# Relative scores of both halves ahead of the attention, norms and slot weights in another order: one change to a twelve-layer decoder kernel

## The chip, the core and the metric

The kernel runs on one core of one Trainium2 chip. The core has a matrix engine (PE, TensorE, with PEld for its weight loads), three engines for elementwise work (DVE or VectorE, ACT or ScalarE, POOL or GpSimd), and SP, which here only issues transfers. Each engine works through its own instructions in a fixed order and waits, where it must, for another engine or for a transfer. PE, DVE, ACT and POOL compute on SBUF; PE writes its products to PSUM[...]. The metric is the device time of one execution in microseconds, lower is better; a kernel is compared by the median of its runs.

## The reference

The input `x` is 16 sequences of 64 tokens of 128 features, 1024 rows. Twelve sublayers follow one another, each added to its input and normalized over the features:

```python
x = _layernorm(x + _L2_ffn_ref(x, ...), axis=-1)    # sw: best of 16 experts, and a shared one
x = _layernorm(x + _L3_attn_ref(x, ...), axis=-1)   # at3: relative positions, causal
x = _layernorm(x + _L3_xattn_ref(x, ctx_1024, ...), axis=-1)  # xa3: attention to ctx
x = _layernorm(x + _L3_ffn_ref(x, ...), axis=-1)    # tt: best two of 8 experts
```

These four are the last ones, and the change lies among them. The attention with relative positions has 16 heads of 8 features. To the product of queries and keys it adds the product of the queries with a table of relative positions, read at a skew: row `q`, column `k` takes entry `k - q + n - 1`.

```python
scores = jnp.einsum('bhqd,bhkd->bhqk', q, k)
scores = scores + jnp.einsum('bhld,lrd->bhlr', q, rel_emb[rel_idx])
scores = jnp.where(causal[None, None], -jnp.inf, scores)
attn = jax.nn.softmax(scores / np.sqrt(HD), axis=-1)
```

The last layer routes each token to its two best experts and weights the two outputs with a softmax of the two logits:

```python
topk_logits, topk_idx = jax.lax.top_k(logits, TOP_K)
w = jax.nn.softmax(topk_logits, axis=-1)
h = gelu(jnp.einsum('th,ehi->tei', xt, W1) + b1)
y = jnp.einsum('te,teh->th', gates, jnp.einsum('tei,eih->teh', h, W2) + b2)
```

## The kernel before

**Halves.** The 1024 rows are two halves `h` of 512, each as four tiles of 128 rows. `self.xt[h]` holds the rows with tokens on the partitions, `self.x[h]` the transpose. Each sublayer ends in `close`: statistics on DVE (L195, L197), the inverse deviation, and a normalization (L206) into a new `xt`. For most layers POOL computes the inverse deviation (L201, L204). For `sw` it is `inverse_deviation`, eleven small DVE steps (L176 to L183) with a scratch tile `pd_sw` in PSUM. `close` returns `flip`: it fills PE with some `keep_busy` matmuls, transposes `xt` on PE (L224) and copies the result to `x[h]` on ACT (L226).

**Order.** A planner places the instructions. For each engine it takes the earliest instruction in program order that its own model of time finds ready; so program order is a priority, and the order on the chip is fixed when the kernel is built. A tile is a named buffer of a pool; a tag with `bufs=n` has n places, and the (n+1)th tile of the tag waits until a place is free. Pools are opened and closed by stage.

**Two streams.** A stage of attention layers is written as two generators, one for each half. `side_by_side` runs the first `lead` steps of half 0 and then steps of both in turn. A step ends at a `yield`. In `attention` the first step of `at3` computes the queries and keys (`at_pq`, `at_pk`, copied by ACT at L429, keys spread over masks by POOL at L441), calls `relative`, computes the values, and does `weights` of the first of four units. A unit is a quarter of the half's scores, 128 by 1024. `weights` computes the scores on PE (L480, with the mask added at L491), adds the relative scores (L533), takes the maximum (L536), subtracts it (L537) and exponentiates on ACT (L540). The following steps take the next units; `turn` transposes a unit (L551), `weigh` multiplies it with the values (L572).

**Relative scores.** For each of the four units `relative` computes the product with the table (`at_rs`), copies it from PSUM (ACT, L659), writes it to memory in two transfers (L663), and reads it back at a skew in four (L673), all through SP's queue. What comes back is a tile of tag `got` with `bufs=4`, which `weights` then uses as its scores and `turn` frees.

**The routed layers.** In `switch_ffn` (`sw`) and `top2_ffn` (`tt`) `place` computes a slot for each token and choice. `tiles_in_step` then works through tiles of 128 slots: POOL gathers the rows of a tile (`fetch`, L1336), PE transposes them (`turn`), `first`, `flip` and `second` are the two products of the tile's expert and what lies between. `between(k)` is called at the head of step k, from k = -1 on. In `tt` it is `weigh`: at k = 0 it computes each slot's weight `ws` and target row `outs` with ten DVE steps, one of ACT (L1572), 16 matmuls (`tt_pw`, L1582) and seven DVE sums; `second(0)`, which is called at k = 2, is the first to use them. After the tiles of `sw`, POOL gathers the tokens' rows (`sw_back`, eight transfers), and for each half DVE adds them to `base` (L1473), and `close(...)()` normalizes and transposes at once. After those of `tt` two reads for each half (`tt_back`, L1640), two additions (L1644) and `close` follow, and the four tiles of each half are stored by SP (L211).

**Where the stages meet.** `run` opens the attention stage's pools after `switch_ffn` has closed its own:

```python
        self.switch_ffn()
        with self.work_pools("a3", {8: 3, 4: 8, 2: 8}):
            self.side_by_side(self.second_stream, 2)
        self.top2_ffn()
```

Of the kernel before, what the change touches and what calls it, by code (L numbers as in the profile page):

```python
# [11 lines left out]
F32 = mybir.dt.float32  # L12
# [9 lines left out]
P = 128  # L22
B, S, D = 16, 64, 128
# [14 lines left out]
class Kernel:  # L38
# [146 lines left out]
    def close(self, pool, h, y, tag, shift=False, ones=0):  # L185

        nc = self.nc
        stats = self.lnp.tile([P, 4, 6], F32, tag=f"stats{h}", name=f"stats_{tag}{h}")  # L190
        mv = self.lnp.tile([P, 4, 2], F32, tag=f"mv{h}", name=f"mv_{tag}{h}")
        rstd = self.lnp.tile([P, 4], F32, tag=f"rstd{h}", name=f"rstd_{tag}{h}")
        xt = self.xp.tile([P, 4, D], F32, tag=f"xt{h}", name=f"xt_{tag}{h}", bufs=1 + h)
        for i in range(4):
            nc.vector.bn_stats(stats[:, i, :], y[:, i, :])  # L195
        for i in range(4):
            nc.vector.bn_aggr(mv[:, i, :], stats[:, i, :])  # L197
        if tag == "sw":
            self.inverse_deviation(rstd, mv, self.psum(pool, f"pd_{tag}{h}"))
        else:  # L200
            nc.gpsimd.tensor_tensor(  # L201
                rstd, mv[:, :, 1], self.eps.to_broadcast([P, 4]), ALU.add
            )
            nc.gpsimd.tensor_tensor(rstd, rstd, self.minus.to_broadcast([P, 4]), ALU.pow)  # L204
        for i in range(4):
            nc.vector.tensor_scalar(  # L206
                xt[:, i, :], y[:, i, :], mv[:, i, 0:1], rstd[:, i : i + 1], ALU.subtract, ALU.mult
            )
            if tag == "tt":
                at = h * HALF + i * P  # L210
                nc.sync.dma_start(  # L211
                    out=self.out.rearrange("b s d -> (b s) d")[at : at + P, :], in_=xt[:, i, :]
                )
        self.xt[h] = xt

        def flip():
            ps = self.psum(pool, f"px_{tag}{h}")
# [190 lines left out]
    def attention(  # L408
# [4 lines left out]
        nc = self.nc  # L413
        work, psc, pt = self.aw, self.psc, self.pt
# [101 lines left out]
        km = km or keys(x)  # L516
        rels = self.relative(tag, rel, q, h, scores) if rel else None
        v = values()
        y = self.new_y(tag, h) if wo is None else None
# [122 lines left out]
    def relative(self, tag, rel, q, h, scores):  # L642
# [12 lines left out]
        for u in range(2):  # L655
            for gp in range(2):
# [3 lines left out]
                mem = self.scratch.tile([2, P, row], F32, tag=f"rel{h}{u}{gp}", name=f"{tag}_mem{h}{u}{gp}")  # L660
                got = work.tile([P, 2, 2, 4, S], F32, tag="got", name=f"{tag}_rel{h}{u}{gp}", bufs=4)
                for pr in range(2):
# [720 lines left out]
    def switch_ffn(self):  # L1383
        nc, tc, x = self.nc, self.tc, list(self.x)
        E = 16
        with (
# [81 lines left out]
            for i in range(8):  # L1468
                self.gather(back[i // 4][:, i % 4, :], self.sw_out, slot[:, i : i + 1])
            for h in range(2):  # L1470
                y = self.new_y("sw", h)
                for i in range(4):
                    nc.vector.tensor_tensor(y[:, i, :], base[h][:, i, :], back[h][:, i, :], ALU.add)  # L1473

                    if h == 0:
                        for n in range(4):
# [3 lines left out]
                            )  # L1480
                self.close(pt, h, y, "sw", ones=4 - 2 * h)()

# [17 lines left out]
    def top2_ffn(self):  # L1500
        nc, tc = self.nc, self.tc
        E = 8
        with (
# [49 lines left out]
            def weigh(k):  # L1553
                if k != 0:
                    return
# [57 lines left out]
            def second(k, e, hid):  # L1613
# [18 lines left out]
                "tt", work, pt, self.tt_in, ids, first, flip, second, weigh, 20  # L1632
            )
            for h in range(2):
                y = self.new_y("tt", h)
                last = self.xt[h]
                for c in range(2):
# [7 lines left out]
                    last = y  # L1645
                self.close(pt, h, y, "tt")

# [119 lines left out]
    def second_stream(self, h):  # L1767
# [3 lines left out]
        def third():  # L1771
# [11 lines left out]
            ),  # L1783
            third,
        )
        self.score(h, "tt", "tt_wg", 8)

    def side_by_side(self, stream, lead):

        ahead, behind = stream(0), stream(1)  # L1790
        for _ in range(lead):
            next(ahead)
        running = [ahead, behind]
        while running:
            running = [half for half in running if next(half, self) is not self]

    def run(self, out):
# [20 lines left out]
        with self.work_pools("a3", {8: 3, 4: 8, 2: 8}):  # L1818
            self.side_by_side(self.second_stream, 2)
        self.top2_ffn()  # L1820
# [191 lines left out]
```

## Time and profile before

| | us |
|---|---|
| median of 3 runs | 896.4 (886.66 to 896.52) |
| profiled execution | 871.75 |
| its span, first to last instruction | 869.8 |
| from the last tile of `sw` to the first product of `at3` (633 to 652.3) | 19.3 |
| `at3` until PE is full (652.3 to 692) | 39.7 |
| from the last product of `xa3` to the first of `tt` (770 to 795.2) | 25 |
| from the last product of `tt` to the end (849 to 869.8) | 21 |

The durations that follow come from the profiled execution, so a sum is set against 871.75 and its span of 869.8. The three runs are longer than it by 1.7 to 2.8%.

How a line of the timeline is read: start, duration, engine, line, operation, output `<-` inputs, shapes of the output and of the first input, and how many instructions were merged (`x4`); in brackets the idle time of that engine before it, and what ended it. `PE` times are those of pipelined matmuls and overlap. A transfer on `SPq` is listed with the time in which SP issued it, not with its landing. Clock is the TensorE clock that was granted, as a share of full speed.

### The profile page before, as it was taken

How to read it: one execution, taken by the hardware profiler on the slowest of the kernel's cores; microseconds unless marked ns; L12 is line 12 of the kernel's file. 1: busy time of each engine (PE TensorE's matmuls, PEld its weight loads, DVE VectorE, ACT ScalarE, POOL GpSimd, SP SyncE). 2: the span in 40 equal slices, each digit the busy share in tenths (PEclk: the TensorE clock that was granted, in tenths of full speed). 3: DMA queues.
4: the chain of work that ended last, by engine and by line, in shares of the span. 5: the costliest groups of instructions: out<-in, count | busy, mean ns of one | idle time of the engine just before them, and what ended most of it. 6: DMA issues, size and time to landing. Idle time of an engine off the chain costs nothing.

```text
span 869.8 us, 17379 instructions
## 1 busy us (share of the span) xinstructions
PE 717.0 (82%) x7045; PEld 455.8 (52%) x7045; DVE 481.7 (55%) x1103; ACT 354.9 (41%) x584; POOL 254.0 (29%) x289
## 2 busy tenths in 40 slices
PE   6777979878888699789996999977947999967990
PEld 2333646555545466546573557644633565744770
DVE  4556466574665745447525766544542565656563
ACT  2223547445454444445551445522304554522330
POOL 2314135070432703130305220016151111025732
PEclk7878989889999998989996989988977799978995
DMA  7900000000000000140000000051115625031102
GB/s 277 273 1 25 2 1 2 14 1 2 1 2 1 1 2 2 40 155 2 2 2 0 1 2 2 2 151 48 50 41 148 198 54 184 2 122 37 53 25 83
DMA packets 34504, 43.65 MB, mean 50 GB/s; under 512 B 7524, under 2 KB 26469, under 8 KB 33784
## 3 DMA queue, kind: packets, MB, share of 16 engines
q1 hardware_dynamic: 32344, 38.26, 14.1%
q0 software_dynamic: 2080, 4.26, 1.7%
q8 instruction: 58, 0.95, 0.5%
q14 instruction: 22, 0.18, 0.1%
HBM read 34.31 MB, written 11.61 MB: 53 GB/s over the span
## 4 chain that ended last, share of the span: by engine, by line
PE 51%; DVE 18%; POOL 9%; issue 6%; ACT 4%; DMA 4%; SPq 1%; DVEq 0%; POOLq 0%; ACTq 0%
PE xa_sc L480 5%; PE xa_av L572 4%; PE xa_pt L551 3%; PE sw_pe L151 2%; PE at_sc L480 2%; PE lb_qk L151 2%; DVE lb_t L818 2%; PE at_av L572 2%; PE xa_sc L491 2%; DMA at_mem<-at_rsb 2%; DVE lb_t L832 2%; PE xa_pt L156 2%; PE at_pt L551 1%; PE lb_pf L868 1%; PE lb_pw L151 1%
## 5 line engine op out<-in xcount | busy, mean ns | idle before, releaser
L536 DVE TENSOR_REDUCE xa_mx<-xa_sc 128x16 f32<-128x1024 f32 x40 | 48.7, 1218 | 63.8 <-PE xa_sc L491 41.4
L838 POOL TENSOR_TENSOR lb_t<-lb_t,lb_t 128x1024 f32<-128x1024 f32 x16 | 37.7, 2357 | 99.4 <-DVE lb_t L832 95.2
L554 ACT COPY xa_eT<-xa_pt 128x512 f32<-128x512 f32 x80 | 45.5, 587 | 40.8 <-PE xa_pt L551 40.0
L540 ACT ACTIVATE xa_e<-xa_e 128x1024 f32<-128x1024 f32 x40 | 42.3, 1058 | 37.2 <-DVE xa_e L537 37.1
L480 PE MATMUL xa_sc<-xa_km,xa_q 32*64 32x256 f32 x640 | 55.2, 404 | 0.7 <-ACT xa_q L431 0.5
L551 PE MATMUL xa_pt<-const,xa_e 128*128 128x128 f32 x320 | 48.8, 280 | 1.8 <-ACT xa_e L540 1.8
L441 POOL TENSOR_SCALAR xa_km<-xa_k,const 128x512 f32<-128x512 f32 x40 | 27.1, 695 | 79.3 <-ACT xa_k L429 46.0
L537 DVE TENSOR_TENSOR xa_e<-xa_sc,xa_mx 128x1024 f32<-128x1024 f32 x40 | 48.7, 1217 | 2.1
L551 PEld LDWEIGHTS xa_pt<-const,xa_e 128*128 128x128 f32 x320 | 40.3, 145 | 13.1 <-ACT xa_e L540 3.7
L572 PEld LDWEIGHTS xa_av<-v,xa_eT 128*64 128x64 f32 x1280 | 40.5, 138 | 8.2 <-issue 6.1
L572 PE MATMUL xa_av<-v,xa_eT 128*64 128x18 f32 (+1 forms) x1280 | 44.2, 209 | 0.0
L156 PEld LDWEIGHTS <-ones_b 128*128 128x128 bf16 x255 | 24.8, 104 | 36.4 <-issue 19.9
L151 PE MATMUL lb_qk<-w,lb_hs 128*128 128x512 f32 x64 | 35.8, 686 | 8.5 <-DVE lb_t L832 4.8
L480 PEld LDWEIGHTS xa_sc<-xa_km,xa_q 32*64 32x64 f32 x640 | 24.7, 136 | 19.9 <-issue 12.8
L814 DVE TENSOR_REDUCE lb_ss<-lb_t 128x16 f32<-128x1024 f32 x16 | 19.5, 1217 | 27.9 <-ACT lb_t L811 27.9
L201 POOL TENSOR_TENSOR rstd_xa<-mv_xa,eps 128x4 f32<-128x4 f32 x8 | 1.6, 201 | 112.2 <-DVE mv_xa L197 112.2
L156 PE MATMUL xa_pt<-ones_b 128*128 128x512 bf16 x80 | 30.2, 390 | 0.0
L862 POOL TENSOR_TENSOR lb_t<-lb_t,lb_rs 128x1024 f32<-128x1024 f32 x16 | 30.1, 1904 | 0.0
L868 PE MATMUL lb_pf<-const,lb_t 128*128 128x128 f32 x128 | 20.1, 312 | 9.4 <-POOL lb_t L862 9.3
L480 PE MATMUL at_sc<-at_km,at_q 32*64 32x256 f32 x256 | 22.5, 452 | 5.2 <-DVE at_rel L533 3.7
L533 DVE TENSOR_TENSOR at_rel<-at_rel,at_sc 128x1024 f32<-128x1024 f32 x8 | 9.7, 1212 | 29.2 <-DMA at_mem<-at_rsb 16.4
L554 ACT COPY at_eT<-at_pt 128x512 f32<-128x512 f32 x32 | 17.6, 586 | 19.3 <-PE at_pt L551 13.4
(474 smaller groups left out, 1715.0 us busy)
## 6 DMA issues: line engine op xcount, KB each, us to landing
sw_gu<-in_sw_gu SPq DMA_DIRECT2D x4, 1024.0 KB, 8.3
at_mem<-at_rsb SPq DMA_DIRECT2D x16, 256.0 KB, 2.9
at_rel<-at_mem SPq DMA_DIRECT2D x32, 128.0 KB, 3.0
w<-in_w SPq DMA_DIRECT2D x1, 3114.0 KB, 12.2
sw_dn<-in_sw_dn SPq DMA_DIRECT2D x4, 512.0 KB, 7.0
tt_w<-in_tt_w SPq DMA_DIRECT2D x2, 1024.0 KB, 8.6
tt_b<-in_tt_b SPq DMA_DIRECT2D x1, 2048.0 KB, 7.1
sw_in<-in_zeros SPq DMA_DIRECT2D x1, 1472.0 KB, 11.6
```

The source lines that it names most:

```text
L151: self.nc.tensor.matmul(out, lhsT, rhs, start=n == 0, stop=n == len(pairs) - 1)
L156: self.nc.tensor.matmul(out, self.ones_b, self.ones_b.unsqueeze(1).to_broadcast([P, 4, P]), start=True, stop=True)
L480: nc.tensor.matmul(sc[64 * j : 64 * j + 64, gg, at : at + 256], q[r, t], part[r, :, t] if local else part[r, :, :], start=not masked or (p ...
L536: nc.vector.tensor_reduce(mx, scored, AX.X, ALU.max)
L537: nc.vector.tensor_tensor(e3, scored, mx.unsqueeze(2).to_broadcast([P, 16, S]), ALU.subtract)
L540: nc.scalar.activation(e3, e3, AF.Exp, scale=scale)
L551: nc.tensor.transpose(ps[:, bass.ts(n, P)], blocks[:, bass.ts(n, P)], self.g("ident"))
L554: nc.scalar.copy(eT[:, gg, :], ps)
L572: nc.tensor.matmul(av[64 * j : 64 * j + 64, pr, hp, :, :], eT[:, gg, at : at + 64], v[:, b, hp, :, :], start=True, stop=True,)
L838: nc.gpsimd.tensor_tensor(t1, t1, t2.rearrange("p t n d -> p t (n d)"), ALU.add)
L862: nc.gpsimd.tensor_tensor(t3, t3, rs[:, bass.ts(r, 16)].unsqueeze(2).to_broadcast([P, 16, 64]), ALU.mult)
L868: nc.tensor.transpose(ps[:, c, :], t1[:, t, bass.ts(c, P)], ident)
```

## The change

Five edits, as one change.

1. `close` is split into `moments` (statistics and inverse deviation) and `normalize` (the normalization and `flip`). Both keep their last instruction, `self.measured` and `self.normed`. `flip` takes the pool of its PSUM tile as an argument.
2. After `sw` half 1 is ended inside `tc.issue_after(self.normed.ins)`: every DVE instruction of half 1 that is traced there comes after half 0's last normalization on DVE. Half 1's `flip` is no longer run there. It is handed to the second stream, which runs it at the start of half 1's first layer, with the new stage's PSUM pool.
3. In `attention` a step ends after `relative`, and `side_by_side` takes a number `both` of steps that both halves do first. With `both=1` in the second stream, queries, keys and relative scores of half 1 come ahead of values and `weights` of half 0. The tag `got` has five places.
4. In `tt` `weigh` does its work at k = 2, right ahead of `second(0)`.
5. At the end of `tt` the moments of both halves come first, then, on DVE behind the last `bn_aggr` of half 1, both normalizations with their stores.

```diff
+        mv, rstd = self.moments(pool, h, y, tag)
+        return self.normalize(pool, h, y, tag, mv, rstd, shift, ones)
+
+    def moments(self, pool, h, y, tag):
...
         for i in range(4):
-            nc.vector.bn_aggr(mv[:, i, :], stats[:, i, :])
+            self.measured = nc.vector.bn_aggr(mv[:, i, :], stats[:, i, :])
...
+        return mv, rstd
+
+    def normalize(self, pool, h, y, tag, mv, rstd, shift=False, ones=0):
+        nc = self.nc
+        xt = self.xp.tile([P, 4, D], F32, tag=f"xt{h}", name=f"xt_{tag}{h}", bufs=1 + h)
         for i in range(4):
-            nc.vector.tensor_scalar(
+            self.normed = nc.vector.tensor_scalar(
...
-        def flip():
+        def flip(pool=pool):
...
         rels = self.relative(tag, rel, q, h, scores) if rel else None
+        if rel:
+            yield
         v = values()
...
-                got = work.tile([P, 2, 2, 4, S], F32, tag="got", name=f"{tag}_rel{h}{u}{gp}", bufs=4)
+                got = work.tile([P, 2, 2, 4, S], F32, tag="got", name=f"{tag}_rel{h}{u}{gp}", bufs=5)
...
-            for h in range(2):
+            def end(h):
                 y = self.new_y("sw", h)
...
-                self.close(pt, h, y, "sw", ones=4 - 2 * h)()
+                return self.close(pt, h, y, "sw", ones=4 - 2 * h)
+
+            end(0)()
+
+            with tc.issue_after(self.normed.ins):
+                flip = end(1)
+
+            self.flips = [None, lambda: flip(self.pt)]
...
             def weigh(k):
-                if k != 0:
+                if k != 2:
                     return
...
+            made = []
             for h in range(2):
                 y = self.new_y("tt", h)
...
-                self.close(pt, h, y, "tt")
+                made.append((h, y, "tt", *self.moments(pt, h, y, "tt")))
+            with tc.issue_after(self.measured.ins):
+                for half in made:
+                    self.normalize(pt, *half)
...
             third,
+            flip=self.flips[h],
         )
...
-    def side_by_side(self, stream, lead):
+    def side_by_side(self, stream, lead, both=0):
...
         ahead, behind = stream(0), stream(1)
+        for _ in range(both):
+            next(ahead)
+            next(behind)
...
-            self.side_by_side(self.second_stream, 2)
+            self.side_by_side(self.second_stream, 2, 1)
```

## The prediction

> **What bounds the kernel now.** I read the page first: the busy times and the chain that ended last.
>
> ```profile
> PE 717.0 (82%) x7045; PEld 455.8 (52%) x7045; DVE 481.7 (55%) x1103; ACT 354.9 (41%) x584; POOL 254.0 (29%) x289
> PE 51%; DVE 18%; POOL 9%; issue 6%; ACT 4%; DMA 4%; SPq 1%; DVEq 0%; POOLq 0%; ACTq 0%
> ```
>
> TensorE is the bound on the whole, but the change touches only stages around the two routed layers, so the share over the span says little. The second view is busy time by stage (us; then PE, PEld, DVE, ACT, POOL; clock, DMA share, GB/s).
>
> ```profile
> 633.00:652.00 19.00, 10.32 (x46) 8.24 (x46) 9.64 (x54) 0.91 (x2) 11.50 (x15) 0.68 0.11 29
> 652.00:668.00 16.00, 11.69 (x138) 5.35 (x138) 0.46 (x1) 7.21 (x10) 3.14 (x5) 0.82 0.36 106
> 668.00:692.00 24.00, 21.30 (x210) 11.66 (x211) 13.02 (x12) 12.11 (x16) 2.98 (x4) 0.71 0.70 204
> 692.00:712.00 20.00, 19.37 (x271) 13.80 (x271) 16.45 (x19) 10.17 (x16) 0.00 (x0) 0.95 0.33 95
> 849.00:870.00 21.00, 0.00 (x0) 0.00 (x0) 7.36 (x29) 0.00 (x0) 4.03 (x6) 0.55 0.26 82
> ```
>
> From 692 on PE is full at clock 0.95; from 633 to 692 it is not, and its clock is 0.68 to 0.82. Those 59 us, and the tail after 849, are where order can be worth something. The third view, the timeline, says who waits there.
>
> ```profile
> 650.00 1.11 DVE L206 TENSOR_SCALAR xt_sw<-y_sw,mv_sw,rstd_sw 128x128 f32<-128x128 f32 x4
> 652.31 2.08 PE L151 MATMUL at_pq<-x_sw,w 128*128 128x512 f32 x2 [0.68 <-ACT x_sw L226]
> 667.54 1.22 DVE L533 TENSOR_TENSOR at_rel<-at_rel,at_sc 128x1024 f32<-128x1024 f32 x1 [16.43 <-DMA at_mem<-at_rsb]
> 671.52 1.22 DVE L533 TENSOR_TENSOR at_rel<-at_rel,at_sc 128x1024 f32<-128x1024 f32 x1 [0.24 <-DMA at_rel<-at_mem]
> 675.74 1.22 DVE L533 TENSOR_TENSOR at_rel<-at_rel,at_sc 128x1024 f32<-128x1024 f32 x1 [0.50 <-DMA at_rel<-at_mem]
> 688.98 1.22 DVE L533 TENSOR_TENSOR at_rel<-at_rel,at_sc 128x1024 f32<-128x1024 f32 x1 [9.49 <-DMA at_rel<-at_mem]
> ```
>
> VectorE waits 16.4 us for the first relative scores, and 9.5 us again at 688.98. That fourth addition belongs to half 1: it stands in DVE's order ahead of half 0's last one (690.74), and its scores were still in memory. The queue that carries them is SP's:
>
> ```profile
> 674.23 3.43 SPq L673 DMA_DIRECT2D at_rel<-at_mem  x4
> 681.50 2.56 SPq L663 DMA_DIRECT2D at_mem<-at_rsb  x4
> 684.16 5.21 SPq L673 DMA_DIRECT2D at_rel<-at_mem  x8
> ```
>
> Half 0 is read back by 677.66. Then SP is empty for 3.8 us, since half 1's product (L480, 678.27) and its copy (L659, 680.48) come only then. From half 1's first write to its addition: 688.98 - 681.50 = 7.5 us.
>
> **The change part by part.** Sums are against the profiled run, 871.75 us (span 869.8 and 1.95 around it). The median of the three runs shown is 896.4, 2.8% longer; I carry the saving over as a share.
>
> *Norms behind the first routed layer.* Now DVE mixes half 1's additions, which wait 0.39, 0.46 and 0.99 us for gathers, into half 0's chain. Afterwards half 0 goes first. Its last addition is at 641.05, its statistics end at 641.95. Eleven steps of inverse_deviation at a pitch of 0.20 (648.19 to 649.80 in eight pitches) reach 644.2, four normalizations (1.11) 645.3, where they now end at 648.08. Half 1 then pays four additions and four statistics (0.27 each, 2.2), aggregates 0.45, eleven steps 2.2: 650.15, and its normalization ends at 651.3 (now 651.11). So half 1 loses 0.2 and half 0 wins 2.8. What is it worth? at_pq of half 0 starts now at 652.31, held by the copy of x_sw of half 1, which it does not read: half 0's copy ended at 649.10. PE's order alone would have released it at 651.64, when half 1's transposes end. So the first tile of the new PSUM pools waits for the last use of the closed ones. Afterwards the transposes and copy of half 1 belong to the new pool, but the scratch of its inverse_deviation still belongs to the old: at_pq can start at about 650.3. Value 2.0; bounds 5.9 (646.4, if only half 0's copy counts) and 0. I take the row's behaviour, a wait for the whole pool.
>
> The moved flip issues two keep_busy, four transposes (1.24) and one copy (0.59); they go behind half 0's product, on PE and ACT. SP and POOL get nothing of it. Here a rule speaks against the change: the Trainium skill, "TensorE: Matmul & The Clock Gate", section "HAM oscillation — how this bites in real kernels", warns of PE gaps above about 3.4 us, after which the array runs at half rate. The deferral leaves PE idle from about 645.9 to 650.3, 4.4 us, where now keep_busy and transposes fall. The row: at_pq takes 2.08 now, xa_pq of the same form 1.12 at 720.64, so it is already at half rate; a gap costs nothing more. By the rule taken alone the pair pq, pk would lose 1.9 us; by the row 0. I take 0.
>
> *Relative scores of both halves first.* For half 1 these move ahead of half 0's values and scores: on PE pq and pk (1.0 to 2.0 each) and four products (0.65 warm, 1.0 cold each); on ACT the copies of q and k (0.59 each) and four of 0.97; on POOL base (1.26) and four km (2.98); on SP 8 writes and 16 reads at 0.61, 14.6 us of queue. Nothing else stands in SP until 714.89 (tt_w) or in POOL until 713.92, so those two delay nobody. ACT does: from 655.4, eight copies of 0.97 and three of 0.59 last until 665.0, the PSUM slots go to half 0's scores then, 1.7 us later they are ready: 666.7. Its first scores come back from memory 2.0 us earlier than now, 665.5. So the first addition is at 666.8, now 667.54. The following two at the larger of DVE's 3.75 per unit (three passes of 1.22 and gaps) and SP's cadence (671.52 to 675.74, 4.2): 670.6 and 674.4, all hidden under transfers.
>
> Then half 1: half 0's reads end on SP at 675.7 (677.66 less 2.0). Half 1's data have been waiting since 665, so its write follows at once; with the same 7.5 us the addition is at 683.2 instead of 688.98. That is 5.8 earlier, the 2.0 included, so 3.8 of its own. What is late next is the same addition's transfer (DVE would be free at 678.2). The remaining reads of half 1 need a buffer freed by half 0's transposes (five buffers instead of four: only the first is free at once); those transposes are at about 672 to 685, and SP has only half 1's own reads behind the wait. From there on the stage is full of PE work (row 692:712) and keeps what it has won.
>
> Second rule, same place: "DMA: Bandwidth & Descriptors", section "Issuing engines are not separate DMA queues", calls a sequencer's time to initiate a DMA "usually small relative to the DMA itself". Were that so here, half 1's unit would go out beside half 0's, land near 675, and DVE would go on at 678.2: 10.8 instead of 5.8. The rows say 0.61 of issue against a median of 3.0 to landing, and 48 of them in one ordered queue: 29 us. I take the row, and keep 10.8 as an end. The other end is a loss of 3: if PE does half 1's products strictly ahead, half 0's scores end near 670.7 and the first addition is 3.3 later.
>
> *Slot weights behind the first tiles.* The 16 matmuls of tt_pw (2.02 us) stand before the first tile's product.
>
> ```profile
> 793.17 2.02 PE L1582 MATMUL tt_pw<-tt_wof,tt_at_row 128*128 128x138 bf16 x16 [1.74 <-issue]
> 795.20 1.65 PE L151 MATMUL tt_ph<-tt_w,tt_xs 128*128 x2
> ```
>
> The first product can start at 793.2 instead (tile 1's gather, issued at 789.66, lands by 792.5 at the 2.85 of tile 0; PE's own issue of 1.74 stays). PE pays the matmuls later, at up to 2.02 cold, half of it warm, partly in the 0.79 us in which PE waits for the first Gelu at 798.61. Ends: 0, if the same gaps are filled as now, and 2.0; value 1.0. The DVE steps of weigh (3 copies, 2 subtractions, 5 products of 0.53, 7 sums) move with it, beside tiles that leave DVE 40% free (33.2 of 54 us busy in 795:849).
>
> *Norms at the end.*
>
> ```profile
> 859.25 1.11 DVE L206 TENSOR_SCALAR xt_tt<-y_tt,mv_tt,rstd_tt 128x128 f32<-128x128 f32 x4 [1.22 <-POOL rstd_tt L204]
> 859.63 6.05 SPq L211 DMA_DIRECT2D out<-xt_tt  x8
> 863.55 1.11 DVE L206 TENSOR_SCALAR xt_tt<-y_tt,mv_tt,rstd_tt 128x128 f32<-128x128 f32 x4 [1.40 <-POOL rstd_tt L204]
> ```
>
> DVE idles 1.22 for POOL's power and normalizes half 0 before half 1's second addition. Afterwards half 1's statistics end at 859.85, POOL's 1.3 us end at 861.2, its normalization starts at 861.25: 2.3 earlier. Half 0's starts at 859.9, so the first of eight stores leaves at 860.25; at SP's pitch of 0.46 the last leaves at 863.5, now 865.3. So SP's queue limits it: 1.8 (between 0.5 and 2.3).
>
> Sum: 2.0 + 3.8 + 1.0 + 1.8 = 8.6 us. 871.75 - 8.6 = 863.2, a ratio of 0.990; 896.4 x 0.990 = 887.5.
>
> **The rivals.** *The queue keeps it (20%).* SP's issue, not the late product, sets half 1's landing: reads that wait for a buffer stretch it, and the 3.8 is nothing. For: only one spare buffer. Against: 3.8 us of empty SP. 4.8 us remain: 866.9, or 891.5.
>
> *PE fills up (20%).* Half 1's scores land early, the 9.5 us stall goes almost wholly and PE comes warm into the stage: 10.8, with 2.0 and 2.3 of the last two parts, and some 2 us of matmuls at full clock (at_sc of 1.98 at 668 to 690 against 1.09 at 694.61, four of them): 17. 854.7, or 879.
>
> *A read that waits stands before others (13%, slower).* If SP's order puts a read of half 1, which needs half 0's first buffer, ahead of half 0's own last reads, SP stops until half 0's first transposes (about 676) and every later unit costs a full 7.5 instead of 4.2: three units, 10 us, against 5.8 + 2.8 of gain. Net 1.4 to 4 slower: about 873 to 876, 898 to 900. It decides from a wait of some 3 us per unit. Against it: program order has all of half 0's reads first.
>
> That the change does not do what it says is likely only for the slot weights: an idle PE may take the same matmuls first. It is in their lower end.
>
> **How the numbers follow.** The forecast has 47%, the rivals 20, 20 and 13. Runs of the same kernel lie between 886.66 and 896.52, so 2% (about what a measurement can tell from no change) is 18 us: the forecast is within it. Faster by over 2%, under 878.5: half of "PE fills up" and a little of the forecast through spread, 0.2. Slower by over 2%, over 914: only if the last rival is worse than worked out, 0.06. The range takes in all four cases with the spread on either side: 869 to 902.
>
> **What would show it.** Right: at_pq near 650; at_rs of half 1 before the first at_sc; SP without a hole between half 0's last read and half 1's first write; the DVE wait of 9.5 down to about 5; tt_ph ahead of tt_pw; stores of the output in one row of eight. Wrong: at_pq still at 652 or already at 646; the first L533 later than 668; SP waiting for transposes amid half 0's reads; the stage from 692 on longer than now.

## The result and the profile after

The changed kernel takes 878.98 us (median of 4 runs, 875.16 to 884.41) against 894.02 (886.66 to 896.52) for the kernel before. The ratio on record is 0.9882, 95% interval 0.9833 to 0.9930; the quotient of the two medians, 0.983, lies at its lower end. Measured again with more runs (experiment 5) the ratio is 0.9909 (0.9886 to 0.9933), about 8 us of 889. The changed kernel is faster by about 1%, no more than single runs of one kernel differ by. Ratios leave out executions that took over 1.5% longer than the fastest of their kernel; the profiled executions of experiments 3 and 10 are of that kind.

The two profiled executions say the opposite at first sight: the span is 882.4 us, and it was 869.8. The busy times of the changed kernel:

```profile
PE 722.0 (82%) x7043; PEld 455.5 (52%) x7045; DVE 483.1 (55%) x1103; ACT 354.3 (40%) x584; POOL 254.9 (29%) x289
```

The work is the same (for the kernel before see the prediction), so the 12.6 us lie in waits and in the clock. A good part of them lies in layers that the change doesn't touch. Busy time from 50 to 100 us, of the kernel before and then of the changed one (us; PE, PEld, DVE, ACT, POOL; clock, DMA share, GB/s):

```profile
50.00:100.00 50.00, 41.90 (x401) 23.41 (x398) 26.52 (x56) 17.86 (x35) 12.78 (x16) 0.84 0.04 12
```

```profile
50.00:100.00 50.00, 42.10 (x320) 22.32 (x317) 25.77 (x54) 15.62 (x31) 12.67 (x15) 0.70 0.04 11
```

In the same 50 us PE got through 320 matmuls instead of 401, at a granted clock of 0.70 instead of 0.84. When the first gather of `sw_back` starts, the changed kernel is already 9.3 us behind (643.14 against 633.86), before anything of the change has run. So two profiled executions can't be set against each other by their spans. From here on every time is counted from an event close by: G is the start of the first gather of `sw_back`, T that of the first gather of `tt_got`.

| us | before | after | exp. 5: after again |
|---|---|---|---|
| G to `at_pq` | 18.5 | 15.6 | 15.8 |
| G to the first addition of relative scores | 33.7 | 37.6 | 34.4 |
| G to the fourth | 55.1 | 49.2 | 48.8 |
| G to the fifth | 56.9 | 53.9 | 53.5 |
| G to the eighth | 73.9 | 70.3 | 70.5 |
| G to half 1's `y_at` | 96.3 | 94.2 | 92.9 |
| T to the first `tt_ph` | 6.9 | 4.1 | 4.2 |
| T to the first scatter | 16.4 | 19.5 | 19.3 |
| T to the last scatter | 61.3 | 69.2 | 69.0 |
| last scatter to the end of the span | 20.2 | 17.9 | 18.3 |

The 8 us in the row "T to the last scatter" don't come from the change: with the slot weights in the old place it was 68.3 to 70.1 in experiments 1, 2, 4 and 6, and 61.3 to 61.4 only in this profile of before and in that of experiment 11 (last section).

Busy time by stage in the changed kernel, the stretches that answer to those shown of before:

```profile
642.28:661.28 19.00, 10.11 (x43) 7.51 (x44) 10.41 (x54) 0.98 (x2) 12.38 (x15) 0.70 0.11 29
661.28:677.28 16.00, 13.10 (x134) 5.72 (x135) 0.00 (x0) 8.64 (x12) 5.38 (x8) 0.71 0.51 153
677.28:701.28 24.00, 20.97 (x279) 12.28 (x272) 17.96 (x17) 13.20 (x18) 0.00 (x0) 0.93 0.77 228
```

The second stretch holds more transfers (153 GB/s, it was 106) and no VectorE at all; in the third VectorE is busy 18.0 of 24 us, where it was 13.0. That is the change at work: relative scores go out early, and the additions then follow closely. Who waits, from the timeline of the changed kernel (first, fourth and fifth addition only):

```profile
658.50 0.16 DVE L183 SCALAR_TENSOR_TENSOR rstd_sw<-pd_sw,rstd_sw 128x4 f32<-128x4 f32 x1
658.76 2.04 PE L151 MATMUL at_pq<-x_sw,w 128*128 128x512 f32 x2 [3.78 <-issue]
680.72 1.22 DVE L544 TENSOR_TENSOR at_rel<-at_rel,at_sc 128x1024 f32<-128x1024 f32 x1 [20.91 <-DMA at_mem<-at_rsb]
692.34 1.22 DVE L544 TENSOR_TENSOR at_rel<-at_rel,at_sc 128x1024 f32<-128x1024 f32 x1 [2.37 <-DMA at_rel<-at_mem]
697.00 1.22 DVE L544 TENSOR_TENSOR at_rel<-at_rel,at_sc 128x1024 f32<-128x1024 f32 x1
```

`at_pq` starts 0.10 us after the last step of half 1's inverse deviation has ended (658.66), as was worked out. The first addition is late: half 1's product and its copies stand ahead of half 0's first scores. The wait of 9.5 us before the fourth is down to 2.4 here, and to 5.0 in experiment 5, where the first addition came earlier.

The slot weights stand behind the first products of two tiles now, and most of the gain is gone a few microseconds later:

```profile
799.49 1.44 PE L151 MATMUL tt_ph<-tt_w,tt_xs 128*128 x2
803.49 1.21 PE L1600 MATMUL tt_pw<-tt_wof,tt_at_row 128*128 128x138 bf16 x16
811.65 2.08 PE L151 MATMUL tt_ph<-tt_w,tt_xs 128*128 x2 [4.24 <-remote]
```

At the end the eight stores leave in one row, and half 1's normalization follows half 0's after 1.5 us, where it took 4.3:

```profile
874.68 1.09 DVE L215 TENSOR_SCALAR xt_tt<-y_tt,mv_tt,rstd_tt 128x128 f32<-128x128 f32 x4
875.02 3.66 SPq L220 DMA_DIRECT2D out<-xt_tt  x8
876.17 1.11 DVE L215 TENSOR_SCALAR xt_tt<-y_tt,mv_tt,rstd_tt 128x128 f32<-128x128 f32 x4 [0.41 <-POOL rstd_tt L208]
```

### The profile page after: what moved, and what is told of

Same layout as the page of the kernel before. It is cut to its first block, busy times and chain, and to the rows that moved or that the text cites. A ratio compares the mean times of both kernels' runs of the same rounds, so it can differ in the third digit from the quotient of the medians.

```text
span 882.4 us, 17386 instructions
## 1 busy us (share of the span) xinstructions
PE 722.0 (82%) x7043; PEld 455.5 (52%) x7045; DVE 483.1 (55%) x1103; ACT 354.3 (40%) x584; POOL 254.9 (29%) x289
## 4 chain that ended last, share of the span: by engine, by line
PE 49%; DVE 17%; POOL 8%; issue 7%; DMA 5%; ACT 5%; another core or an unknown queue 1%; SPq 1%; POOLq 0%; DVEq 0%; ACTq 0%
PE xa_sc L489 5%; PE xa_av L583 4%; PE xa_pt L562 4%; PE sw_pe L151 2%; DVE lb_t L829 2%; PE lb_qk L151 2%; DVE lb_t L843 2%; PE xa_sc L500 2%; PE xa_pt L156 2%; PE at_pt L562 1%; PE at_av L583 1%; PE at_sc L489 1%; DMA at_mem<-at_rsb 1%; PE tt_ph L151 1%; PE lb_pw L151 1%
## 5 line engine op out<-in xcount | busy, mean ns | idle before, releaser
L547 DVE TENSOR_REDUCE xa_mx<-xa_sc 128x16 f32<-128x1024 f32 x40 | 48.8, 1219 | 67.2 <-PE xa_sc L500 44.7
L562 PE MATMUL xa_pt<-const,xa_e 128*128 128x128 f32 x320 | 51.3, 291 | 1.8 <-ACT xa_e L551 1.8
L562 PEld LDWEIGHTS xa_pt<-const,xa_e 128*128 128x128 f32 x320 | 42.4, 151 | 14.2 <-ACT xa_e L551 3.7
L156 PEld LDWEIGHTS <-ones_b 128*128 128x128 bf16 x255 | 24.7, 105 | 35.7 <-issue 19.5
L825 DVE TENSOR_REDUCE lb_ss<-lb_t 128x16 f32<-128x1024 f32 x16 | 19.5, 1217 | 27.4 <-ACT lb_t L822 27.4
L879 PE MATMUL lb_pf<-const,lb_t 128*128 128x128 f32 x128 | 18.9, 299 | 10.1 <-POOL lb_t L873 10.0
L151 PE MATMUL tt_ph<-tt_w,tt_xs 128*128 x40 | 22.9, 657 | 4.2 <-remote 4.2
L1347 POOL DMA_INDIRECT tt_got<-tt_in,tt_ids x20 | 19.6, 978 | 18.8 <-DVE tt_ids L1324 6.6
L1640 POOL DMA_INDIRECT tt_out<-tt_ys,tt_outs x20 | 19.5, 977 | 18.8 <-DVE tt_ys L1639 15.2
```

Source lines behind the costliest of these rows:

```text
L151: self.nc.tensor.matmul(out, lhsT, rhs, start=n == 0, stop=n == len(pairs) - 1)
L156: self.nc.tensor.matmul(out, self.ones_b, self.ones_b.unsqueeze(1).to_broadcast([P, 4, P]), start=True, stop=True)
L547: nc.vector.tensor_reduce(mx, scored, AX.X, ALU.max)
L562: nc.tensor.transpose(ps[:, bass.ts(n, P)], blocks[:, bass.ts(n, P)], self.g("ident"))
```

## The experiments

Ratios are against the kernel before, run on the same chip. Experiments 1 to 4 each keep one part of the change and undo the other three; they shared their runs of before (median 889.21).

**1. Only the norms behind `sw`** (the last lines of `switch_ffn` and `flip=` in the second stream as in the change).

> Only the norms behind the first routed layer are reordered (half 1's additions behind half 0's normalization, half 1's transposes behind half 0's product); everything else as before. Theory (the sum of the parts holds, and this part is worth what the profile of the changed kernel shows): from the first gather of sw_back to at_pq 15.6 us instead of 18.45 (-2.9), and the same 2.9 still there at half 1's y_at; ratio 0.997. Rival (this part only moves the wait): at_pq comes 2.9 earlier, but half 1's transposes and its product of x_sw now stand where half 0's work was, and the first addition of relative scores and half 1's y_at are no earlier than before relative to the gather (33.7 and 96.3 us); ratio 1.000.

Ratio 0.9967 (0.9938 to 0.9995). `at_pq` at 16.0 us (2.4 earlier than in the kernel before), first addition at 30.4 (3.3 earlier), half 1's `y_at` at 94.1 (2.2 earlier). The theory holds in kind, with 2.2 to 2.4 us for its 2.9; the rival, which had the gain lost by the first addition, falls.

**2. Only the relative scores first.**

```diff
         rels = self.relative(tag, rel, q, h, scores) if rel else None
+        if rel:
+            yield
...
-                got = work.tile([P, 2, 2, 4, S], F32, tag="got", name=f"{tag}_rel{h}{u}{gp}", bufs=4)
+                got = work.tile([P, 2, 2, 4, S], F32, tag="got", name=f"{tag}_rel{h}{u}{gp}", bufs=5)
...
-            self.side_by_side(self.second_stream, 2)
+            self.side_by_side(self.second_stream, 2, 1)
```

> Only the relative scores of both halves are put first (with the fifth buffer); both halves are normalized and transposed as before. Theory: half 1's product ahead of half 0's scores delays the first addition by some 3 to 4 us against the gather (37 instead of 33.7 us) and yet the wait of 9.5 us for half 1's first unit falls to 3 or less, so that the last of the eight additions comes 0 to 4 us earlier than 73.9 us behind the gather; ratio 0.995 to 0.999. Rival (this part carries most of the measured 1.2%: TensorE keeps busy and warm through the stage): the last addition 7 us earlier or more, ratio 0.990. Other rival (the queue keeps it): last addition not earlier, ratio 1.000 or above.

Ratio 0.9950 (0.9921 to 0.9980). First addition at 37.8, fourth at 51.9, eighth at 70.4 (3.5 earlier), `y_at` at 92.9 (3.4 earlier). The theory holds: the first addition pays 4.1 us and the part still wins. The rival that all of the gain is here falls.

**3. Only the slot weights** (`k != 2` in `weigh`).

> Only the slot weights are moved behind the second tile's first product. Theory: the first product starts 6.9 - 4.1 = 2.7 us earlier against the first gather of tt_got (4.1 instead of 6.9 us), but the first tile's result needs the weights all the same, so the first scatter comes no more than 1 us earlier than 16.4 us behind the gather and the last one 0 to 2 us earlier than 61.3 us; ratio 0.998 to 1.000. Rival (the stall seen in the profile of the changed kernel, where from 807.4 to 811.2 no semaphore of TensorE advanced, belongs to this order): it shows here again, the last scatter 4 us or more later; ratio 1.005. Second rival: all 2.7 are kept to the end; ratio 0.997.

Ratio 1.0007 (0.9981 to 1.0034). First product at 4.3 us, first scatter at 19.3, last at 68.3. In experiments 1, 2 and 4, on the same chip and with the weights in the old place, these were 6.9, 20.3 to 22.0 and 68.3 to 70.1. So the product is early, the first scatter still is by 1 us or more, and the last one is not. The second rival, that all 2.7 us are kept, would make 0.997, below the interval. The wait in TensorE's completions shows here again: VectorE and ScalarE stand still together for 6.5 us, until 15.6 us behind T. But in the old order on this chip they do so for 1.7 to 2.7 us, until 13.4 to 15.6, so the wait isn't bound to the new order; it begins earlier there and ends no later. No last scatter came later for it.

**4. Only the tail** (`moments` of both halves ahead of both normalizations).

> Only the norms at the end are reordered. Theory: the eight stores leave in one row and from the last scatter to the end of the span it takes 17.9 us instead of 20.2; ratio 0.9975. Rival (the stores' queue or their landing sets the end): 19.5 us or more; ratio 0.999 to 1.000.

Ratio 1.0000 (0.9971 to 1.0029). From the last scatter to the end 18.5 us, 1.8 less than before (17.9 was expected). The profile shows the gain at the step that was worked out; 0.2% of the time is smaller than this interval, which takes in the theory's 0.9975 and the rival's 1.000 alike. By time it stays open.

**5. The changed kernel again.**

> The changed kernel once more, unaltered. Theory (the parts add up: 0.9967 for the norms, 0.995 for the scores, 1.0007 for the weights, 1.000 for the tail): ratio 0.992. Rival (together they bring more than apart, as the first measurement of 0.988 has it: half 1's transposes fill TensorE's wait): 0.988. In its profile the stage from the first gather to half 1's y_at takes 94 us (96.3 before), and from the first gather of tt_got to the last scatter 68 to 70 us, where the profiled execution of before had 61.3: that execution was then an unusually short one in a stretch that the change hardly touches.

Ratio 0.9909 (0.9886 to 0.9933), 22 runs. The product of the four parts, 0.9924, lies in it; the rival's 0.988 does not. `y_at` is at 92.9, a little better than expected, and the tiles take 69.0.

**6. The changed kernel with the slot weights back in front** (`k != 0`).

> The changed kernel with the slot weights put back in front of the tiles. Theory (the 2.7 us that the first product gains are lost again before the first scatter): the same time as the changed kernel within 0.2%, first product at 6.9 us behind the first gather instead of 4.1, last scatter at 68 to 70 us behind it in both. Rival (the moved weights cost the wait of 4 us in TensorE's completions that two profiles showed at 12 us behind the gather): 2 to 3 us faster than the changed kernel, last scatter at 65 to 66. Second rival (they are worth their 2.7): 2 to 3 us slower.

Ratio 0.9869 (0.9809 to 0.9928), the same as experiment 5 within the intervals. First product at 6.9, last scatter at 68.7. The theory holds by the last scatter, which the first rival had at 65 to 66. By time this experiment alone can't tell 2 us; together with experiment 3 it leaves no gain and no loss that could be measured.

**7. Half 1's scratch in another place.**

```diff
-            self.inverse_deviation(rstd, mv, self.psum(pool, f"pd_{tag}{h}"))
+            pd = self.lnp.tile([P, 8], F32, tag="pd", name=f"pd_{tag}{h}") if h else self.psum(pool, f"pd_{tag}{h}")
+            self.inverse_deviation(rstd, mv, pd)
```

> The changed kernel with the scratch of half 1's inverse_deviation in a tile of SBUF instead of the closing PSUM pool. Theory (the first product of the second attention waits for the last use of the closed pool, and that is this scratch): at_pq starts at 12.7 us behind the first gather instead of 15.6, and the first addition of relative scores follows by 1 to 3 us; ratio 0.001 to 0.003 below the changed kernel's. Rival (something else holds at_pq as well, half 1's additions from the closing SBUF pool or TensorE's own order): at_pq at 15 or later, same ratio.

Ratio 0.9844 (0.9794 to 0.9894), more than the expected 0.003 below experiment 5. `at_pq` is at 12.6, as computed. Timeline of this kernel:

```profile
652.01 1.12 PE L151 MATMUL at_pq<-x_sw,w 128*128 128x512 f32 x2 [0.68 <-ACT x_sw L236]
652.98 1.02 PE L151 MATMUL at_pk<-x_sw,w 128*128 128x512 f32 x2
656.11 0.63 DVE L181 SCALAR_TENSOR_TENSOR pd_sw<-rstd_sw,pd_sw 128x4 f32<-128x4 f32 x1
654.71 2.69 POOL L451 TENSOR_SCALAR at_km<-at_k,const 128x512 f32<-128x512 f32 x4
```

The product follows half 0's copy of `x_sw` at once, while half 1's inverse deviation still runs (until 18.2 us). It takes 1.12 us, not 2.04: PE was idle for 0.68 us before it, not 3.78, and the granted clock (third number from the right) is 1.00 here, where it was 0.50 in the changed kernel. First the stretch of the changed kernel with this product, then that of this one:

```profile
656.76:663.50 6.74, 4.74 (x28) 1.98 (x36) 2.70 (x14) 1.17 (x2) 3.02 (x7) 0.50 0.00 0
```

```profile
646.30:666.70 20.40, 14.88 (x168) 7.86 (x168) 11.06 (x46) 10.08 (x13) 12.38 (x18) 1.00 0.39 114
```

`y_at` comes at 86.3, 6.6 us earlier than in experiment 5: twice the gain at `at_pq`.

**8. Half 1's relative scores one step later.**

```diff
         for _ in range(both):
             next(ahead)
+            next(ahead)
             next(behind)
-        for _ in range(lead):
+        for _ in range(lead - both):
             next(ahead)
```

> The changed kernel with half 1's relative scores one step later: behind half 0's values and its first unit of scores, ahead of the second. Theory (in the changed kernel half 0's first addition is late by 3.9 us because half 1's product and its copies stand ahead of half 0's first scores, and from there on VectorE works without a pause, 32.7 us for eight units, so that this delay is paid in full): first addition at 31 to 34 us behind the first gather instead of 37.6, last one at 67 or earlier instead of 70.3, half 1's y_at at 91 to 92 instead of 94.2; ratio 0.003 below the changed kernel's. Rival (half 1's first unit is then late again): a wait of 5 us or more ahead of the fourth addition, the last one at 70 or later, same ratio.

Ratio 0.9838 (0.9781 to 0.9894). First addition at 29.6, fourth at 50.6 after a wait of 1.4, eighth at 67.8, `y_at` at 90.2, 2.7 earlier than in experiment 5. The rival falls. The end of the stage came about as expected, but not by the path expected: the second addition is late instead (41.8; 36.7 in experiment 5). The delay by half 1's product moved behind the first unit and costs less there. The medians, 873.85 against 880.68 us in experiment 5 on the same chip, differ by more than these 2.7; where the rest is won isn't shown.

**9. Half 1's transfers from another queue.**

```diff
+        queue = nc.gpsimd if (tag, h) == ("at3", 1) else nc.sync
...
-                    nc.sync.dma_start(
+                    queue.dma_start(
```

> The changed kernel with half 1's 24 transfers of relative scores issued by GpSimd instead of SP. Theory (half 1's first unit comes at 49 us behind the gather because its six transfers stand in SP's one ordered queue behind half 0's 24, which go out without a hole from 21.7 us on): fourth addition at 44 to 45 us instead of 48.8 to 49.2, half 0's last read out by 38 us instead of 42, half 1's y_at 1 to 3 us earlier than 93 to 94 us; ratio 0.002 lower than the changed kernel's 0.991. Rival (GpSimd issues more slowly than SP, about 1 us for each as in the gathers, and TensorE's products set the fourth addition): fourth addition at 48 or later, ratio 0.991 or above.

Ratio 0.9946 (0.9920 to 0.9972), where the changed kernel had 0.9909 on another chip: no gain that shows. The fourth addition stays at 49.0, the third moves from 40.4 to 45.6, and half 1's `y_at` is at 92.0 (92.9 in experiment 5). What the transfers took (KB, us from issue to landing), first in experiment 5, then here:

```profile
at_mem<-at_rsb SPq DMA_DIRECT2D x16, 256.0 KB, 3.0
at_rel<-at_mem SPq DMA_DIRECT2D x32, 128.0 KB, 2.9
```

```profile
at_mem<-at_rsb SPq DMA_DIRECT2D x8, 256.0 KB, 3.5
at_rel<-at_mem SPq DMA_DIRECT2D x16, 128.0 KB, 4.0
at_mem<-at_rsb POOLq DMA_DIRECT2D x8, 256.0 KB, 6.1
at_rel<-at_mem POOLq DMA_DIRECT2D x16, 128.0 KB, 4.9
```

and busy time by stretch, first of experiment 5, then of this kernel, 38 us behind G in both:

```profile
678.80:686.80 8.00, 6.17 (x92) 4.31 (x92) 5.71 (x5) 4.25 (x6) 0.00 (x0) 1.00 0.72 214
```

```profile
675.20:683.20 8.00, 3.02 (x42) 1.82 (x34) 2.18 (x3) 1.64 (x2) 2.86 (x5) 0.81 1.04 337
```

The second queue filled the 16 DMA engines (share 0.72 to 1.04, 214 to 337 GB/s), and each transfer took longer, those left on SP too. (How much of the 6.1 us from GpSimd's queue is due to that queue itself was not separated.) What that did to the units, from the timeline of this kernel (half 1's first writes and reads; third and fourth addition):

```profile
667.46 4.35 POOL L675 DMA_DIRECT2D at_mem<-at_rsb  x6
671.34 2.88 POOL L685 DMA_DIRECT2D at_rel<-at_mem  x4
682.79 1.22 DVE L544 TENSOR_TENSOR at_rel<-at_rel,at_sc 128x1024 f32<-128x1024 f32 x1 [5.82 <-DMA at_rel<-at_mem]
686.20 1.21 DVE L544 TENSOR_TENSOR at_rel<-at_rel,at_sc 128x1024 f32<-128x1024 f32 x1
```

Half 1's first unit did come earlier. Its first write left 30.3 us behind G (39.8 in experiment 5), and its four reads, issued from 34.2 on, took 6.6 to 7.1 us to land, so the unit was there by about 43 (an estimate from these numbers), where experiment 5 had VectorE wait for it until 48.8. But half 0's third unit, which stands ahead of it in VectorE's order, was now late: VectorE waited 5.8 us for the third addition and not at all for the fourth. So the theory is right that SP's queue holds half 1's first unit in the changed kernel, and wrong that the fourth addition would follow it: what the second queue gave to half 1 it took from half 0. The rival had the right result by a wrong reason, since GpSimd issued at 0.7 us each (six in 4.35), hardly slower than SP.

The ratio can't be put down to this stage alone. From the last scatter to the end this kernel took 21.0 us, against 18.0 in experiment 10 on the same chip with the same tail; why isn't shown.

**10. Experiments 7 and 8 together.**

> The two edits that gained, together: half 1's scratch in SBUF and half 1's relative scores behind half 0's first unit. Theory (they act at different places, the start of the stage and the first addition): at_pq at 12.6 us behind the first gather, first addition at 27, half 1's y_at at 84 to 86; ratio 0.977 to 0.981. Rival (both only feed SP's queue earlier, and from the fourth addition on the stage is the same): half 1's y_at at 86 to 90, ratio 0.983 to 0.985.

Ratio 0.9832 (0.9781 to 0.9883), `at_pq` at 12.6, first addition at 25.4, eighth at 63.6, `y_at` at 86.0. The rival holds: at the eighth addition and at the end it is the stage of experiment 7 (63.9, 86.3). The first addition, 6.8 us earlier than there, brings nothing more.

**11. The kernel before with half 1's scratch in SBUF** (the diff of experiment 7 in the kernel before; profile only).

> The kernel before with nothing changed but half 1's scratch in SBUF. Theory (a first tile of the new pools waits for the last use of the closed ones, and before that is half 1's copy of x_sw, not the scratch): at_pq at 18.4 us behind the first gather or later, as before, since the copy stays where it is and the scratch is only slower in SBUF. Rival (the scratch itself held the product in both kernels): at_pq at 16 or earlier.

`at_pq` at 19.3 us, right behind half 1's copy of `x_sw`:

```profile
655.86 2.07 PE L151 MATMUL at_pq<-x_sw,w 128*128 128x512 f32 x2 [0.68 <-ACT x_sw L227]
```

The theory holds: it is whatever use of the closed pool comes last.

**12. Four buffers instead of five** (`bufs=4`).

> The changed kernel with four buffers for the relative scores instead of five, so that half 1's first unit has no free one and waits for half 0's first transposes. Theory (the fifth buffer matters little: the transfers of half 0 last until 42 us behind the first gather, and half 0's first transposes free a buffer at 41 to 43 us): fourth addition at 49 to 51 us, where it is at 48.8 to 49.2 with five, half 1's y_at at 93 to 95 us, ratio within 0.002 of the changed kernel's 0.991. Rival (the early order is worth nothing without the free buffer): fourth addition at 53 us or later, the wait ahead of it 8 us or more, ratio 0.995 or above.

Ratio 0.9872 (0.9834 to 0.9910), no worse than experiment 5 (on another chip). Two additions in one row of its timeline:

```profile
693.67 2.35 DVE L544 TENSOR_TENSOR at_rel<-at_rel,at_sc 128x1024 f32<-128x1024 f32 x2 [7.90 <-DMA at_rel<-at_mem]
```

The fourth addition is at 53.2, 4.3 us later than with five buffers, after a wait of 7.9: both numbers are the rival's. But `y_at` is at 93.0 (92.9 with five), as the theory has it, and the time, lower than either of them said, is nearer to the theory's. The fifth addition follows at once (54.3), and what VectorE left undone it does without a pause. Where the fourth addition stands says little of where the stage ends.

## Why the prediction was right, and where it was not

The forecast was a ratio of 0.990; 0.9882 and 0.9909 were measured. The terms of the sum, one by one:

*Norms, 2.0 us: right in mechanism and about in size.* The claim was that the first product of the new pools waits for the last use of the closed ones. In every run with the reordered norms and the scratch in PSUM `at_pq` started 0.10 us after the last step on `pd_sw`; with the scratch elsewhere (experiment 7) it fell to 12.6, and the prediction's lower end, if half 0's copy alone counts, was 646.4 - 633.9 = 12.5. In the kernel before the last use is a copy, and it held there too (experiment 11). The gain at `at_pq` is 2.4 to 3.0, and in experiment 1 it is 2.2 at the end of the stage.

The rule weighed there was that of the Trainium skill, "TensorE: Matmul & The Clock Gate", section "HAM oscillation — how this bites in real kernels": PE gaps above about 3.4 us halve the rate, -1.9 for the pair of products. Against the kernel before the row was right, 2.04 against 2.08. But experiment 7 shows the rule's price at the same place: behind a gap of 0.68 instead of 3.78 the two products take 1.12 and 1.02 instead of 2.04 and 1.91, 1.8 us. The row of before hid it, because the clock was low there already, and not because of this gap of 0.68. The granted clock had been 1.00 from 642.9 on and fell at 649.7, 2.6 us ahead of the product:

```profile
649.70:656.50 6.80, 5.43 (x16) 2.26 (x24) 1.34 (x6) 1.54 (x3) 1.26 (x1) 0.50 0.00 0
```

PE's longest gap between 642.9 and this fall was 3.0 us, and in the changed kernel the clock fell at 656.8, less than 2 us into the gap of 3.78. So the rule gives the price here, but its length of a gap does not say when it is paid.

*Scores, 3.8 us: the place of the fourth addition right, its worth not.* It was put at 683.2, that is 49.3 behind G; 48.8 to 49.2 were measured, with a wait of 5.0 in experiment 5 where "about 5" stood. The step that failed is "From there on the stage is full of PE work (row 692:712) and keeps what it has won". Of the 5.8 us that norms and scores had together, 3.4 were left at the fifth addition, the eighth and half 1's `y_at` (2.2 in the first profile). Before, the late fourth addition had the fifth right behind it (1.8 us); now they are 4.7 apart, with other VectorE passes between them. Such a wait is partly made good by what has piled up behind it, which experiment 12 shows without the rest: 4.3 us later at the fourth addition, 0.1 at `y_at`.

The first addition was expected at 666.8, 32.9 behind G. It came at 34.4, and at 37.6 in the first profile: "later than 668", which had been named as a sign that the step is wrong. What was given as the other end, PE doing half 1's products strictly ahead, is what happened, though the stage did not lose by it: in the changed kernel's order on PE all four `at_rs` of half 1 stand ahead of half 0's first `at_sc`, and in experiment 2 the first addition is 4.1 late. The forecast had half 1's copies on ACT counted, but only as far as the PSUM places, not the order on PE.

The reason given for the time of half 1's unit, SP's one ordered queue, holds, but the number is in part luck. In experiment 5 the first copy of that unit ended 29.5 behind G and its first write left SP at 39.8, behind 22 of half 0's 24 transfers. The forecast had the write at 675.7, which is 41.8, and 7.5 us from there to the addition; it took 9.0. The two misses cancel. Experiment 9 confirms the reason, since from another queue the unit came earlier, and shows what the forecast's end of 10.8 left out. The rule was read for its clause on issue time only (the Trainium skill, "DMA: Bandwidth & Descriptors", section "Issuing engines are not separate DMA queues"). Its first sentence counts as well: transfers of all issuing engines run on the same 16 DMA engines. With half of the issues taken from SP the DMA share was 1.04 and half 0's third unit 5 us later.

Of the rivals, "The queue keeps it" was right that SP's queue sets half 1's landing, and wrong that nothing is won. The one in which reads that wait for a buffer stop SP did not occur, since all but two of half 0's reads stand ahead of half 1's first write.

*Slot weights, 1.0 us: mis-sized, it is 0 in the experiments that isolate it.* The first product did come 2.7 us earlier (2.0 expected). Of this 1 us or more is left at the first scatter (19.3 in experiments 3 and 5, 20.3 to 22.0 with the old order) and nothing at the last, and by time it is 1.0007 (0.9981 to 1.0034). The lower end of the term, 0, was right. On the chip of experiments 9 to 11 the last scatter was earlier with the new order, 59.8 and 60.7 against 61.4; three single executions don't settle it.

*Tail, 1.8 us: right in the profile,* 1.8 to 2.3 from the last scatter to the end in every profile with the new tail but that of experiment 9. Time alone couldn't show it.

The terms as the profiles show them, 3.4 for norms and scores, 0 and 2.0, make 5.4 us; 8.1 were measured (6.0 to 10.1). What makes up the difference isn't shown. Part of it may lie in the profile of before: experiment 4, whose kernel leaves this stage as it was, had `y_at` at 97.5 instead of 96.3. Single executions differ by more than the difference, as the first 100 us did, with another clock. That the sum of 8.6 came so close is in part luck: two terms were too large by what the profiles show, and what takes their place in the measured time isn't known.

"PE fills up" was not this change. Experiment 7 comes nearer to it: `at_pq` 3.1 us earlier and PE at full clock for the first products, 6.6 us at the end of the stage. But its clock is 0.50 again from 27 to 44 us behind G, so the warm stage of that rival isn't there either. Experiments 7, 8 and 10 are faster than both kernels, 0.983 to 0.984 against 0.991; their intervals end at 0.988 to 0.989, where that of experiment 5 begins.

## What to carry to other kernels

Where a stage begins with new pools, look for the last use of the closed ones, however small: eleven steps on a 128x8 scratch held a whole stage for 3 us, and the matrix engine began it at half its clock. A wait in the middle of a chain isn't worth its length; count the work that has piled up behind it, and read the gain where the stage ends. Before moving transfers to another queue, look at the share of the DMA engines and at the order in which the results are used: here, at a share of 0.72 to 0.85, the second queue's transfers came earlier and the first one's later, and the later ones were needed first.

## What the runs showed of the hardware

A DVE step on the small scratch takes 0.13 to 0.17 us in PSUM. In SBUF it took up to 0.63 in experiment 7 while GpSimd worked on `at_km` (its line above), and in experiment 11 one step took as long as the GpSimd instruction beside it:

```profile
651.05 1.26 DVE L183 SCALAR_TENSOR_TENSOR rstd_sw<-pd_sw,rstd_sw 128x4 f32<-128x4 f32 x1
651.03 1.26 POOL L165 TENSOR_TENSOR base_at<-xt_sw,wide 128x512 f32<-128x512 f32 x1 [0.67 <-DVE pd_sw L182]
```

That is the exclusive lock which "SBUF — State Buffer" of the Trainium skill describes, section "SBUF: two separate sides": a DVE step with two inputs in SBUF and a GpSimd instruction that reads SBUF don't run together, and the one that starts second waits for the whole of the other. In the changed kernel, with the scratch in PSUM, the steps kept to 0.16 to 0.17 us beside GpSimd's work on `at_relm`.

The tiles of the last layer start differently from chip to chip. In all profiles but those of before and of experiments 9 to 11 there is a stretch of 1.7 to 6.8 us, between 9 and 16 us behind T, in which VectorE and ScalarE stand still, although TensorE's records go on for a part of it. In the profile of the changed kernel no semaphore of TensorE advanced between 803.7 and 811.2, and only then VectorE took the slot weights, whose matmuls stand in the records at 803.49:

```profile
811.25 0.18 DVE L1604 COPY tt_ws<-tt_pw 128x23 f32<-128x23 f32 x1 [6.84 <-remote]
```

From T to the last scatter it took 68.0 to 70.1 us in these profiles, with both places of the slot weights. On the chip of experiments 9 to 11 it was 59.8 to 61.4, and the kernel before had a median of 875 us there, 889 to 890 in the other experiments. By these numbers the profiled execution of before, 61.3 and 871.75, looks like one of the second kind, and the runs of 886 to 897 beside it like the first. What causes the stretch wasn't tried.
